# The second element's h on ScalarE's queue, and its transposition ahead of the sixth output product

## The chip, the cores and the metric

The kernel runs on one core of a Trainium2 chip. The metric is the device time of one execution in microseconds (us), as the median of several runs. The core's engines are named as the profile names them: PE is TensorE (PEld its weight loads), DVE is VectorE, ACT is ScalarE, POOL is GpSimd, and SP is SyncE, whose queue only issues transfers here.

## The reference

The input x holds 64 elements (graphs) of 256 nodes with 512 features in float32; adj is one 256 x 256 adjacency matrix for all of them. Two layers follow each other.

```python
# layer 0
mi = x @ Wi.T;  mj = x @ Wj.T          # W = [Wi | Wj], 512 x 1024
h = layernorm(x + deg * (mi + b) + a @ mj)
# layer 1: attention of 8 heads of 64, masked by adj
q, k, v = h @ Wq.T + bq, h @ Wk.T + bk, h @ Wv.T + bv
attn = softmax(where(adj == 0, -inf, q k^T / 8))
out = layernorm(h + (attn v) @ Wo.T + bo)
```

Each element is independent of the others. h of an element, 256 x 512, is needed in two forms: with nodes on the partitions, as the sum to which layer 1 is added (the tile xh), and with features on the partitions, as the operand of the products for q, k and v (the tile hT).

## The kernel before

**Pairs.** The elements are worked in pairs (NB = 2), numbered g; b1 is a pair's first element and b2 its second. A product with one of Wq, Wk, Wv, Wo for a pair is a 512 x 512 by 512 x 512 product, split into 2 x 2 blocks and done with seven block products in place of eight, after a scheme with sums of blocks. The lists o, q, k, v hold these seven steps each (o for the output product with Wo of pair g, the others for pair g+1). Each step is eight matmuls into one bank of PSUM and then the reading of that bank by another engine. Blocks of the left operand are quarters of hT (or of aoT, the attention's result), and their four sums hS (or oS), which DVE makes in four steps (L477 to L480). The right operands, blocks or sums of blocks of the weights, are not kept: each step takes the next `factor` tile, which SP's queue has loaded from DRAM, eight ahead. The order of these loads follows the list `queue`.

**Banks.** The steps share three PSUM banks, taken in turn (tile `st`, or `po` in layer 0). Step 1 and step 3 of a product go to one bank: step 1 is read out to a kept tile (u), and then step 3 adds to the same bank. So PE may start step 3 only when u has been read. The second and third entries of each list are exchanged (`second_late`), so that o[1], q[1] and k[1] are such third steps.

**One pass of the main loop** (g from 0 to 30) works on pair g's attention and output product, and in between on layer 0 of pair g+1, whose steps come from `layer0`. The last part of the pass, around the change, is

```python
run([o[0], neighbours, take1, take0, q[0], give1, send1, o[1], k[0], give0, send0, multiply,
     *left_steps(oS[g], in_order), q[1], k[1]])
run(o[2:6] + work[SLOTS + 2] + [v[0], o[6], v[1]])
```

Here `neighbours` is the product with the graph for b2 of pair g+1, `take1` and `take0` add it and take the statistics of the norm for the two halves of 128 nodes, and `give1` and `give0` apply the norm on ACT (L466 makes the shift, L467 scales the half of xh): after L467 the half is h. `send1` and `send0` are calls of `send_h` for the two halves, and `work[SLOTS + 2]` is one call of `turn_h`.

**The way of h from xh to hT** has four steps. `send_h` writes each half of h to DRAM, in blocks of 128 columns (tile h_cols, one transfer of 256 KB a half, L599). After the second half it reads all of it back as 512 KB (tile hB, L603), so that a DVE transposition of 32 x 32 blocks (`turn_h`, L485, in `transposed`) gives hT. For a pair's second element `turn_h` then makes the sums hS. hT's second half is first needed by q[2], the sums by q[3].

**Order.** A scheduler places each engine's instructions. Those wrapped in `in_order` (all of PE's, and many others) stay on their engine in the order in which they are written; others it places where it expects them to be ready. An engine and a queue work their instructions off in the order that results. All transfers are issued by SP's queue.

**Reading the banks here.** k[0] is read by ACT as `u<-st,bk`, q[1] as `qT<-st,bq`, k[1] as `kT<-st,bk` (L711, two instructions each). Each of o[2] to o[6] is read by DVE at L740, which adds it to xh; that of o[5] is twice as long, as it is added in two places.

Of the kernel before, what the change touches and what calls it, by code (L numbers as in the profile page):

```python
# [16 lines left out]
P = 128  # L17
# [207 lines left out]
def unshifted_path(ctx, tc, flag, x, adj, wiT, wjT, b0, wqT, bq, wkT, bk, wvT, bv, woT, bo, out):  # L225
# [16 lines left out]
    nc = tc.nc  # L242
# [4 lines left out]
    R = 32  # L247
    NB = 2
    NG = B // NB
    H = D // 2  # L250
    SLOTS = NB * NC // 2
# [44 lines left out]
    xh = {}  # L296

    def load_x(b):
        if b < B:
            xh[b] = p6.tile([P, NT, D], F32, tag="xh", name="xh")  # L300
            nc.sync.dma_start(out=xh[b], in_=x[b].rearrange("(t p) d -> p t d", p=P))

    b_bc = p4.tile([P, D], F32, tag="u", name="b_bc")
    xB, hB = {}, {}
# [37 lines left out]
    a = p2.tile([P, NT, N], F32, tag="pe", name="a")  # L342
# [30 lines left out]
    def add_bias(b):  # L373
        in_order(nc.gpsimd.tensor_tensor(xh[b], xh[b], degb, ALU.add))
# [101 lines left out]
    def left_steps(f, order=anywhere):  # L476
        return [lambda: order(nc.vector.tensor_add(f["S1"], f["A21"], f["A22"])),  # L477
                lambda: order(nc.vector.tensor_sub(f["S2"], f["S1"], f["A11"])),  # L478
                lambda: order(nc.vector.tensor_sub(f["S3"], f["A11"], f["A21"])),
                lambda: order(nc.vector.tensor_sub(f["S4"], f["A12"], f["S2"]))]  # L480
# [112 lines left out]
    h_cols = {}  # L593

    def send_h(b, t):
        i = b % NB
        if t == 1:
            h_cols[b] = dram.tile([D // P, N, P], F32, tag=f"h{i}", name="h_cols")
        nc.sync.dma_start(out=h_cols[b][:, t * P:(t + 1) * P, :].rearrange("q p n -> p q n"),  # L599
                          in_=xh[b][:, t, :].rearrange("p (q n) -> p q n", n=P))  # L600
        if t == 0:
            hB[b] = p1.tile([P, N // R, P], F32, tag="hB", name="hB")
            nc.sync.dma_start(out=hB[b].rearrange("p a n -> p (a n)"),  # L603
                              in_=h_cols[b].rearrange("q (r a) n -> (q r) (a n)", r=R))

    def turn_h(b):
        g, i = divmod(b, NB)
# [60 lines left out]
    def second_late(steps):  # L668
        return [steps[0], steps[2], steps[1], *steps[3:]]
# [30 lines left out]
    def qk_steps(g, store, tag, bias, diff, early=False):  # L700

        def new_store():
            store[g] = p1.tile([P, NC, NB * N], F32, tag=tag, name=tag)

        def place(i, j):
            return store[g][:, 2 * j:2 * j + 2, i * N:(i + 1) * N]

        def biased(b):
            def evict(dst, ps):
                for m in range(2):  # L710
                    nc.scalar.activation(dst[:, m, :], ps[:, m, :], AF.Identity, bias=b[:, m:m + 1], scale=1.0)  # L711
            return evict

        def last(dst, ps, addend):
            for m in range(2):
                nc.vector.scalar_tensor_tensor(dst[:, m, :], ps[:, m, :], diff[:, m:m + 1],
                                               addend[:, m, :], ALU.add, ALU.add)

        return qkv_steps(g, True, new_store, place, biased(bias), biased(diff), last, early)

    def v_steps(g, early=False):
        def new_store():
            vv[g] = p1.tile([P, NB, NT, D], F32, tag="v", name="v_sb")

        def place(i, j):
            return vv[g][:, i, :, j * H:(j + 1) * H]

        def copy(dst, ps):
            nc.scalar.copy(dst, ps)

        return qkv_steps(g, False, new_store, place, copy, copy, nc.vector.tensor_add, early)
# [59 lines left out]
    def scores(g, w):  # L791


        i, pr = divmod(w, NC)
        n0 = i * N
        ps = score_banks("ps").rearrange("p j (t q) -> p j t q", t=NT)
        for kc in range(NT):
            for j in range(2):
                rows = slice(j * DH, (j + 1) * DH)
                matmul(ps[:, j, kc, :], kT[g][rows, pr, n0 + kc * P:n0 + (kc + 1) * P],  # L800
                       qT[g][rows, pr, n0:n0 + N], start=True, stop=True)

        def exponentials():
            pe = p2.tile([P, 2, NT, N], F32, tag="pe", name="pe")
            nc.vector.tensor_add(  # L805
                pe.rearrange("p j t q -> p j (t q)"), ps.rearrange("p j t q -> p j (t q)"),
                maskT.rearrange("p t q -> p (t q)").unsqueeze(1).to_broadcast([P, 2, NT * N]))
            flat = pe.rearrange("p j t q -> p (j t q)")
            in_order(nc.scalar.activation(flat, flat, AF.Exp, scale=QSCALE,  # L809
                                          accum_out=etot[:, NB * g + i, pr:pr + 1]))  # L810
            pk = p3.tile([P, 2, N], F32, tag="pk", name="pk")
            nc.gpsimd.tensor_tensor(pk, pe[:, :, 0, :], pe[:, :, 1, :], ALU.add)  # L812
            made[g, w] = pe, pk

        return exponentials
# [10 lines left out]
    def values(g, w):  # L826
        i, pr = divmod(w, NC)
        if w == 0:
            aoT[g] = p1.tile([P, NC, NB * N], F32, tag="aoT", name="aoT")
            oS[g] = pair_blocks(aoT[g], "oS")  # L830
        pp = w % 2
        if pp == 0:
            pavs[g] = value_bank("pav").rearrange("p (r q) -> p r q", r=2)
        pe, _ = made[g, w]
        for kc in range(NT):
            for j in range(2):
                h0 = (2 * pr + j) * DH
                matmul(pavs[g][j * DH:(j + 1) * DH, pp, :], vv[g][:, i, kc, h0:h0 + DH], pe[:, j, kc, :],
                       start=(kc == 0), stop=(kc == NT - 1))

    def multiply():
        while products:
            d, spread = products.pop()
            in_order(nc.gpsimd.tensor_tensor(d, d, spread, ALU.mult))

    def divide_two(g, w):

        dst = target(g, w)
        nc.scalar.copy(dst, pavs[g])
        divide(dst, [made.pop((g, w - 1))[1], made.pop((g, w))[1]])  # L850
# [44 lines left out]
    def layer0(g):  # L895

        b1, b2 = NB * g, NB * g + 1

        def item(f, *args):
            return lambda: f(*args)  # L900

        p, q = l0_steps(b1), l0_steps(b2)
        return [p[:3] + [item(turn_x, b2)] + p[3:4],
                p[4:7] + [item(sum_x, b2), item(add_bias, b2)] + q[:1],
                p[7:10], p[10:] + q[1:3],
                q[3:6] + [item(turn_h, b1)] + q[6:7],
                q[7:], [item(turn_h, b2)]]

    def run(steps):
        for s in steps:  # L910
            s()
# [4 lines left out]
    def order_of(name):  # L916
        return [(name, n) for n in RIGHT]

    for g in range(-1, NG - 1):
        o, q, k, v = (order_of(name) for name in ("wo", "wq", "wk", "wv"))  # L920
# [18 lines left out]
    p, q = l0_steps(0), l0_steps(1)  # L939
# [18 lines left out]
    o = second_late(qk_steps(0, qT, "qT", bq_sb, bqd, True))  # L958
    k = second_late(qk_steps(0, kT, "kT", bk_sb, bkd, True))
    v = second_late(v_steps(0, True))  # L960
# [21 lines left out]
    for g in range(NG - 1):  # L982
        load_x(NB * (g + 2))
        load_x(NB * (g + 2) + 1)
        work = layer0(g + 1)
        run(work[0])
        for w in range(2, NB * NC, 2):
            values(g, w - 2)
            values(g, w - 1)
            multiply()  # L990
            divide_two(g, w - 1)
            scores(g, w)()
            if w == 4:
                run(work[2])
            later = scores(g, w + 1)
            later()
            run(work[w // 2 if w < 4 else w // 2 + 1])
        w = NB * NC - 2
        values(g, w)
        values(g, w + 1)  # L1000
        multiply()
        o = o_steps(g)
        q = second_late(qk_steps(g + 1, qT, "qT", bq_sb, bqd))
        k = second_late(qk_steps(g + 1, kT, "kT", bk_sb, bkd, True))
        v = second_late(v_steps(g + 1, True))
        neighbours, take1, take0, give1, send1, give0, send0 = work[SLOTS + 1]
        divide_two(g, w + 1)
        run([o[0], neighbours, take1, take0, q[0], give1, send1, o[1], k[0], give0, send0, multiply,
             *left_steps(oS[g], in_order), q[1], k[1]])
        run(o[2:6] + work[SLOTS + 2] + [v[0], o[6], v[1]])  # L1010
        end = finish_steps(g)
        k = with_output_bias(g + 1, k)[2:]
        run(q[2:5] + end[:1] + q[5:6] + end[1:2] + q[6:7] + end[2:3] + k[:1] + end[3:4] + k[1:] + end[4:] + v[2:3])
        turn_x(NB * (g + 2))
        sum_x(NB * (g + 2))
        if g + 2 < NG:
            add_bias(NB * (g + 2))
        run(v[3:5])
        run([scores(g + 1, 0), scores(g + 1, 1)])
        run(v[5:])  # L1020
# [93 lines left out]
```

## Time and profile before

| | |
|---|---|
| median of 3 runs | 3117.25 us (3113.67 to 3117.7) |
| the profiled execution: its span, first to last instruction | 3114.5 us |
| TensorE's granted clock in it | 0.999 |
| PE busy | 3066.7 us (98%) |
| DVE, ACT, POOL busy | 71%, 31%, 48% |
| transfers of h_cols, hB | 124 of 256 KB, 62 of 512 KB, all issued by SP |
| from issue to landing, median | h_cols 2.4 us, hB 3.6 us |

The profiled execution has no other time of its own than the span; what lies around it is in the runs' times alone. Times in the profile's views are counted from the span's start. In a timeline a line has the start, the length, the engine, the source line and the operation with its tiles; instructions of one kind that follow each other are merged (x2, x8), and a bracket gives the idle time before them and what ended it. In a list of waits the columns are the sum, the number and the longest. SPq and ACTq mean the engine's queue, in which transfers are issued. Line numbers are those of the kernel before; in the changed kernel those from L599 on stand two lines later.

### The profile page before, as it was taken

Reading aid. Unit: us, or ns where it says so; the run is one execution under the profiler, and the core shown is the slowest. Engines: PE = TensorE matmul, PEld = TensorE weight load, DVE = VectorE, ACT = ScalarE, POOL = GpSimd, SP = SyncE. Lnnn points to the kernel's source line nnn. Section 1 sums busy time; section 2 is a strip of 40 time slices with the busy share of each in tenths; the row PEclk is TensorE's granted clock in tenths of the full one; section 3 lists DMA queues with packets and bytes.
Section 4 is the critical chain, followed back from the end, with each engine's and each line's share of the span. In section 5 each row is a group of like instructions: output and inputs, shape, how many; then the busy total and the mean of one; then the engine's idle time right before and its main releaser. Section 6 shows DMA issues by size and latency. Waiting matters only on the chain. (4 is left out here: it accounts for less than half of the span.)

```text
span 3114.5 us, 42683 instructions
## 1 busy us (share of the span) xinstructions
PE 3066.7 (98%) x14598; PEld 2125.4 (68%) x14598; DVE 2200.1 (71%) x3298; ACT 967.4 (31%) x1861; POOL 1505.3 (48%) x1255
## 2 busy tenths in 40 slices
PE   8999999999999999999999999999999999999998
PEld 4667766677766777666776667776677766677665
DVE  6776677766777767777667776677766777767775
ACT  2322333323333323332233332333332333323332
POOL 2544445544545445454454554454543545445453
PEclk9999999999999999999999999999999999999999
DMA  7355544455444555345553445544455444555333
GB/s 253 116 151 156 166 122 131 133 155 165 143 123 125 157 165 152 117 129 151 156 166 119 129 135 158 164 142 124 124 159 164 144 123 125 158 158 158 119 106 103
DMA packets 410395, 447.28 MB, mean 144 GB/s; under 512 B 40896, under 2 KB 300224, under 8 KB 409792
## 3 DMA queue, kind: packets, MB, share of 16 engines
q1 hardware_dynamic: 410176, 444.50, 48.4%
q8 instruction: 120, 1.97, 0.3%
q14 instruction: 99, 0.81, 0.1%
HBM read 340.79 MB, written 70.25 MB: 132 GB/s over the span
## 5 line engine op out<-in xcount | busy, mean ns | idle before, releaser
L461 POOL TENSOR_TENSOR rstd<-ve,mhalf 128x1 f32<-128x1 f32 x256 | 140.4, 552 | 715.8 <-DVE below L459 715.8
L812 POOL TENSOR_TENSOR pk<-pe 128x512 f32<-128x512 f32 x256 | 322.5, 1276 | 327.6 <-ACT pe L809 327.5
L290 PE MATMUL po<-w,xS 128*128 128x512 f32 x1024 | 462.4, 599 | 0.4 <-DVE xS L478 0.4
L290 PE MATMUL st<-hS,factor 128*128 128x256 f32 x2048 | 453.5, 380 | 5.1 <-DVE xh L740 3.8
L290 PEld LDWEIGHTS st<-hS,factor 128*128 128x128 f32 x2048 | 388.9, 190 | 60.1 <-DVE xh L740 6.4
L809 ACT ACTIVATE pe<-pe 128x1024 f32<-128x1024 f32 x256 | 270.9, 1058 | 379.0 <-DVE pe L805 379.0
L290 PE MATMUL po<-w,xT 128*128 128x512 f32 x768 | 354.5, 605 | 13.1 <-DVE xT L485 11.1
L290 PE MATMUL st<-hT,factor 128*128 128x256 f32 x1536 | 352.6, 380 | 0.7 <-ACT hT L622 0.7
L290 PEld LDWEIGHTS po<-w,xS 128*128 128x128 f32 x1024 | 190.1, 191 | 235.9 <-issue 206.4
L805 DVE TENSOR_TENSOR pe<-ps,maskT 128x1024 f32<-128x1024 f32 x256 | 298.1, 1195 | 35.3 <-PE ps L290 35.3
L290 PEld LDWEIGHTS st<-hT,factor 128*128 128x128 f32 x1536 | 292.2, 190 | 41.7 <-ACT hT L622 0.9
L882 DVE RECIPROCAL rden<-den 128x256 f32<-128x256 f32 x127 | 223.1, 1757 | 92.2 <-PE den L290 89.0
L290 PEld LDWEIGHTS po<-w,xT 128*128 128x128 f32 x768 | 144.7, 192 | 181.2 <-issue 163.3
L290 PE MATMUL ps<-qT,kT 64*128 64x256 f32 x2048 | 265.0, 393 | 0.0
L290 PE MATMUL pav<-pe,v_sb 128*64 128x256 f32 x2048 | 250.2, 386 | 1.9 <-ACT pe L809 1.8
L883 POOL TENSOR_TENSOR rtot<-rtot,rden 128x256 f32<-128x256 f32 x127 | 92.3, 727 | 329.7 <-DVE rden L882 329.7
L740 DVE TENSOR_TENSOR xh<-st,xh 128x512 f32<-128x512 f32 x186 | 144.6, 777 | 136.4 <-PE st L290 136.4
L290 PEld LDWEIGHTS pav<-pe,v_sb 128*64 128x64 f32 x2048 | 135.3, 136 | 154.0 <-issue 95.4
L290 PEld LDWEIGHTS ps<-qT,kT 64*128 64x128 f32 x2048 | 184.7, 187 | 77.8 <-issue 51.3
L290 PE MATMUL st<-factor,hS 128*128 128x256 f32 x1024 | 234.8, 383 | 0.0
L525 POOL TENSOR_TENSOR lo<-mj,hi 128x512 fp32r<-128x512 f32 x128 | 175.2, 1378 | 107.3 <-ACT hi L524 107.3
L290 PE MATMUL st<-factor,oS 128*128 128x256 f32 x992 | 224.3, 380 | 0.0
(115 smaller groups left out, 4679.5 us busy)
## 6 DMA issues: line engine op xcount, KB each, us to landing
xB<-in_x_dram SPq DMA_DIRECT2D x256, 128.0 KB, 3.8
xh<-in_x_dram SPq DMA_DIRECT2D x64, 512.0 KB, 4.2
factor<-wq SPq DMA_DIRECT2D x128, 256.0 KB, 4.3
factor<-wk SPq DMA_DIRECT2D x128, 256.0 KB, 3.0
factor<-wv SPq DMA_DIRECT2D x128, 256.0 KB, 2.7
spread<-rden SPq DMA_DIRECT2D x1016, 32.0 KB, 1.9
factor<-wo SPq DMA_DIRECT2D x124, 256.0 KB, 3.2
h_cols<-xh SPq DMA_DIRECT2D x124, 256.0 KB, 2.4
```

The lines of the kernel that those rows point to most:

```text
L290: in_order(nc.tensor.matmul(*args, **kw))
L461: nc.gpsimd.tensor_tensor(rstd, ve, mhalf, ALU.pow)
L525: nc.gpsimd.tensor_tensor(k["lo"][:, t, :], k["mj"][:, t, :], k["hi"][:, t, :].bitcast(F32), ALU.subtract)
L740: nc.vector.tensor_add(dst, src, dst)
L805: nc.vector.tensor_add(pe.rearrange("p j t q -> p j (t q)"), ps.rearrange("p j t q -> p j (t q)"), maskT.rearrange("p t q -> p (t q)").uns ...
L809: in_order(nc.scalar.activation(flat, flat, AF.Exp, scale=QSCALE, accum_out=etot[:, NB * g + i, pr:pr + 1]))
L812: nc.gpsimd.tensor_tensor(pk, pe[:, :, 0, :], pe[:, :, 1, :], ALU.add)
L882: nc.vector.reciprocal(rden, den)
L883: nc.gpsimd.tensor_tensor(rtot, rtot, rden, ALU.add)
```

## The change

For a pair's second element, the two writes and the read of `send_h` are issued by ACT instead of SP, and are kept in the written order of ACT's instructions. The first element's stay on SP as they were. And the call of `turn_h` moves from behind o[5] to in front of it.

```diff
         if t == 1:
             h_cols[b] = dram.tile([D // P, N, P], F32, tag=f"h{i}", name="h_cols")
-        nc.sync.dma_start(out=h_cols[b][:, t * P:(t + 1) * P, :].rearrange("q p n -> p q n"),
-                          in_=xh[b][:, t, :].rearrange("p (q n) -> p q n", n=P))
+        queue_of = nc.scalar if i == NB - 1 else nc.sync
+        in_order_of = in_order if i == NB - 1 else anywhere
+        in_order_of(queue_of.dma_start(out=h_cols[b][:, t * P:(t + 1) * P, :].rearrange("q p n -> p q n"),
+                                       in_=xh[b][:, t, :].rearrange("p (q n) -> p q n", n=P)))
         if t == 0:
             hB[b] = p1.tile([P, N // R, P], F32, tag="hB", name="hB")
-            nc.sync.dma_start(out=hB[b].rearrange("p a n -> p (a n)"),
-                              in_=h_cols[b].rearrange("q (r a) n -> (q r) (a n)", r=R))
+            in_order_of(queue_of.dma_start(out=hB[b].rearrange("p a n -> p (a n)"),
+                                           in_=h_cols[b].rearrange("q (r a) n -> (q r) (a n)", r=R)))
...
-        run(o[2:6] + work[SLOTS + 2] + [v[0], o[6], v[1]])
+        run(o[2:5] + work[SLOTS + 2] + [o[5], v[0], o[6], v[1]])
```

In the built program this is the order on ACT in each of the 31 passes; the lines with a plus are new, the others as before:

```
  shift, xh      L466, L467: first half of h
+ h_cols<-xh     first write
  u<-st,bk x2    reads k[0]
  shift, xh      second half of h
  qT<-st,bq      reads q[1], first half
+ h_cols<-xh     second write
  qT<-st,bq      second half
  kT<-st,bk x2   reads k[1]
+ hB<-h_cols     the read, which waits until both writes have landed
  u<-st          reads v[0]
```

On DVE the transposition `hT<-hB` stands in front of the long L740 (that of o[5]) instead of behind it; the sums of hS follow that L740 as before. The orders of PE and POOL are the same. SP's has the three transfers less.

## The prediction

> **What bounds the kernel now.** I read the page's first part, then the waits of TensorE (PE), then the timeline of one pass on each engine.
>
> ```profile
> span 3114.5 us, 42683 instructions
> ...
> PE 3066.7 (98%) x14598; PEld 2125.4 (68%) x14598; DVE 2200.1 (71%) x3298; ACT 967.4 (31%) x1861; POOL 1505.3 (48%) x1255
> ```
>
> PE is busy 98%: it sets the end, and only what makes PE wait, or stops making it wait, counts. Its waits are few (total, times, longest):
>
> ```profile
> PE pa L290 <- POOL lo L525: 15.9, 31, 0.5
> PE po L290 <- DVE xT L485: 11.1, 2, 8.3
> PE st L290 <- DVE xh L740: 3.8, 5, 1.2
> ```
>
> The first is a constant 0.5 us in each of 31 passes, the second belongs to the start. Only the third lies in the change's place. In the trace a pass takes 95.73 to 95.8 us from one first `st<-factor,oS` product to the next, except for seven of 30, longer by 0.1 to 1.8 us. Six of them are those in which VectorE (DVE) waits for hB (`DVE hT L485 <- DMA hB<-h_cols: 5.5, 6`, in the waits). Summing each product's delay over its best pass gives 5.8 us: **all that an earlier h can win**.
>
> The pass that starts at 1209.36 is a usual one. DVE (start, length):
>
> ```profile
> 1213.01 0.69 DVE L740 TENSOR_TENSOR xh<-st,xh 128x512 f32<-128x512 f32 x1 [1.04 <-PE st L290]
> 1214.74 1.23 DVE L740 TENSOR_TENSOR xh<-st,xh 128x1024 f32<-128x1024 f32 x1 [1.03 <-PE st L290]
> 1215.88 2.09 DVE L485 STREAM_TRANSPOSE hT<-hB 128x1024 f32<-128x1024 f32 x1
> ...
> 1220.54 0.68 DVE L740 TENSOR_TENSOR xh<-st,xh 128x512 f32<-128x512 f32 x1
> ```
>
> Behind the transposition come the four sums of hS (1218.00 to 1220.62) and the last L740, for o[6]. Its end, 1221.23, frees the bank of q[3], whose weights load at 1221.28: no room. SyncE's queue (SP), which issues the transfers:
>
> ```profile
> 1204.86 0.38 SPq L599 DMA_DIRECT2D h_cols<-xh  x1
> 1205.33 0.46 SPq L442 DMA_DIRECT2D factor<-in_woT_dram  x1
> 1205.88 0.44 SPq L442 DMA_DIRECT2D factor<-in_wvT_dram  x1
> 1206.41 0.43 SPq L442 DMA_DIRECT2D factor<-wq  x1
> 1206.93 0.38 SPq L599 DMA_DIRECT2D h_cols<-xh  x1
> ...
> 1211.52 0.33 SPq L603 DMA_DIRECT2D hB<-h_cols  x1
> ```
>
> The second write's 512-byte packets start only at 1209.4, behind three factor loads of the same queue, and it lands 4.6 us after its issue, where the first needed 2.4. The read lands at 1215.3, 0.6 us before DVE takes it. ScalarE (ACT) and PE in this place:
>
> ```profile
> 1204.02 0.81 ACT L467 ACTIVATE xh<-xh,shift,rstd 128x512 f32<-128x512 f32 x1
> 1204.74 0.82 ACT L711 ACTIVATE u<-st,bk 128x256 f32<-128x256 f32 x2
> 1205.45 0.29 ACT L466 ACTIVATE shift<-below,rstd 128x1 f32<-128x1 f32 x1
> 1205.77 0.81 ACT L467 ACTIVATE xh<-xh,shift,rstd 128x512 f32<-128x512 f32 x1
> 1206.49 0.82 ACT L711 ACTIVATE qT<-st,bq 128x256 f32<-128x256 f32 x2
> 1207.83 0.84 ACT L711 ACTIVATE kT<-st,bk 128x256 f32<-128x256 f32 x2 [0.53 <-PE st L290]
> ```
>
> ```profile
> 1202.45 5.34 PE L290 MATMUL st<-hT,factor 128*128 128x256 f32 x24
> 1207.63 1.89 PE L290 MATMUL st<-factor,aoT 128*128 128x256 f32 x8
> ```
>
> The 24 products are k[0], q[1], k[1], eight each, 0.2157 us apart: k[1] starts at 1202.45 + 16 x 0.2157 = 1205.90, its weights at 1205.69. It adds to the bank that u(bk) empties, so it must wait for u(bk), which ends at 1205.56: **0.13 us of room**. ACT is 31% busy on the page, but here it runs back to back.
>
> **What the Trainium skill says.** "Perfetto Trace Analysis", section "DMA Instruction — HWDGE (DVE, Sync)": such an instruction is profiled from the moment its semaphores are met, and only at its end is the sequencer free for the next. The trace agrees on SP: h writes take 366 to 384 ns and the next issue starts after them (1204.86, then 1205.33). "DMA: Bandwidth & Descriptors", section "Queues, rings and completion order": SP and ACT each own a row of rings on the same 16 DMA engines, and an engine alternates between rows packet by packet. All 444.50 MB of the data went through one queue, so no run here shows this yet.
>
> **The change part by part.**
>
> 1. *First h write on ACT,* between L467 and u(bk). It waits for L467, which ends at 1204.83; a wait of ACT for itself costs 0.034 us (shift to xh in the trace). Then 0.37 us of issue, taken from SP's row since ACT issues no transfer before. So u(bk) starts at 1205.24, or 1205.32 with the 0.08 us that lie between SP's issues, instead of 1204.74: 0.50 to 0.58 later. PE's room takes 0.13 to 0.2 (at the weights, and a little in the pipeline: in late passes a bank freed 0.28 us late cost 0.24). Left: 0.30 to 0.45 us a pass; I take 0.38, times 31 = **+11.8 us**. Bounds: 0 if the issue overlaps ACT's work; about 0.8 x 31 = 25 us if it is twice as dear as on SP.
> 2. *Second write on ACT.* L467 now ends at about 1207.1. The write is behind the first half of qT, whose execution it can overlap; issue near 1207.15, 0.2 later than now. The rest of qT ends by 1208.0; the bank is needed at 1209.14. Cost 0, hidden by 1.1 us of slack; at an issue of twice the length still 0.
> 3. *hB's read on ACT,* behind kT. It holds ACT until the second write has landed; behind it stands only the copy of v[0]'s bank, not before 1216.46. Cost 0 unless it waits some 5 us.
> 4. *SP loses three transfers,* 93 x 0.36 = 33 us of issue and the waits on xh and h_cols. Its factor loads move up by 0.5 to 1.7 us; they run eight ahead, so PE gains nothing. POOL issues no transfer and keeps its order.
> 5. *Landing of h.* In a queue of its own the second write no longer stands behind the loads; its 512 packets, 27 ns each in the trace, need 512/16 x 27 ns = 0.9 us alone, up to 1.8 if every second packet is another's. From 1207.15 plus 0.8 to the first packet it lands near 1210.0 to 1210.5 (now 1211.5). The read then takes 3.6 to 4.4 us, because factor loads run beside it: 1213.8 to 1215.0.
> 6. *Transposition ahead of o[5]'s L740.* The earliest start is behind L740 of o[4], 1213.01 + 0.69 = 1213.70 (plus 0.38 for PE's shift). But what follows grows by that L740, 1.14 us: hB must land by 1215.88 - 1.14 = 1214.74, or 1215.1 with PE 0.38 later, where 1215.9 sufficed. By step 5 a usual pass meets it: the 5.8 us go. I leave 1.5 us for late passes. o[5]'s own bank is wanted only by q[2] at 1219.5; freed near 1217.3 it costs 0.
>
> Sum: 11.8 - 5.8 + 1.5 = +7.5 us on the profiled 3114.5, so 3122.0. The median of the runs, 3117.25, lies 2.75 above this span, so I expect **3125** us as a median.
>
> **The rivals.**
>
> *The issue on ACT is hidden (not slower).* If ACT's sequencer issues the transfer while ACT is still inside L467, or in under 0.1 us, u(bk) keeps its place and only the gain is left: 3117.25 - 5.8 = 3111.5, with a part of the stall up to 3119. It decides at about 0.15 us of delay to u(bk). For it: ACT's low busy share. Against: the write needs all of L467, and the row of 0.37 us.
>
> *hB lands too late for its new place.* If the two queues only share the bandwidth and the read lands when it does now (median 6.2 us after the pass's first oS product, 1215.55), it misses 1215.1 by 0.43 us in most passes: 13.3 us, and the late passes cost their 5.8 again. 3117.25 + 11.8 + 13.3 = 3142. For it: the 16 DMA engines are busy at 0.75 to 1.1 of their time, by the trace's packets, from 1206 to 1211. Against: they are nearly idle around 1204 and 1212, and h waits for a place in the queue, not for bandwidth. It decides at a landing of 1215.1.
>
> *ACT's issue is dearer than SP's,* 0.8 us: 3117.25 + 25 - 5.8 = 3137. For it, nothing but that ACT's issue is not on record.
>
> *The change does not do what it says:* the built order has the transfers on ACT and the transposition one place earlier in all 31 passes, so no.
>
> **How the numbers follow.** A measurement here can tell about 0.2% from no change, 6.2 us: below 3111.0 is faster, above 3123.5 slower. Forecast 0.58, own range 3120 to 3129, two thirds of it above the bound (0.40 slower, 0.18 same). Hidden issue 0.20 (0.17 same, 0.03 faster: its full gain is just under the bound). Late hB 0.17 and dear issue 0.05, slower. Together 0.03, 0.35, 0.62. The range leaves out the full gain and the worst of late hB: 3113 to 3137.
>
> **What would show it.** Right: a new PE wait of `st` on ACT's u(bk), 31 times, 0.2 to 0.4 us; PE's wait on L740 gone or nearly; u(bk) 0.5 us behind the end of L467 with the issue between; the transposition starting within 0.1 us of its predecessor's end; writes landing under 3.5 us after issue. Wrong: no wait on u(bk) (hidden issue), or DVE waiting for hB in most passes (late hB), or an issue row far from 0.37 us. A time under 3113 breaks step 1, one over 3137 steps 1 or 5.

## The result, and the profile after

The changed kernel took 3128.88 us (median of 5 runs, 3126.03 to 3130.18), the kernel before 3116.09 us beside it (5 runs, 3113.67 to 3117.7): a ratio of 1.0049, 95% interval 1.0036 to 1.0061. It is slower by 12.8 us; 3125 was forecast. The profiled span grew from 3114.5 to 3126.6 us, by 12.1. Where they lie, read from the starts of the passes: 30 passes are longer by 0.36 us on average (10.8), the start up to the first pass is longer by 1.8 (0.4 of it the same stall; the rest lies in the loading of the start, where the kernels shown here differ by up to 4 us), and the end is shorter by 0.6.

The waits of PE and of its weight loads (PEld) after the change:

```profile
PE pa L290 <- POOL lo L525: 15.8, 31, 0.5
PE po L290 <- DMA w<-in_wiT_dram: 9.3, 1, 9.3
PE st L290 <- DVE xh L742: 3.0, 5, 1.1
```

```profile
PEld st L290 <- ACT u L713: 15.8, 31, 0.5
PEld st L290 <- DVE xh L742: 6.5, 9, 1.5
```

The constant wait for `lo` is as before, and the 9.3 us for the first weights stand where the start waited 11.1 us for xT. The new thing is in the second list only: 31 weight loads wait for u(bk), one in each pass. PE's own list does not have it, because a matmul is shown 0.38 us long while they follow each other every 0.2157 us; a gap that pushes the next one by 0.27 us leaves only 0.1 us of idle time to see. ACT's timeline in the pass that starts at 1215.82:

```profile
1210.12 0.81 ACT L467 ACTIVATE xh<-xh,shift,rstd 128x512 f32<-128x512 f32 x1
1210.96 0.37 ACTq L601 DMA_DIRECT2D h_cols<-xh  x1
1211.37 0.84 ACT L713 ACTIVATE u<-st,bk 128x256 f32<-128x256 f32 x2 [0.44 <-ACT xh L467]
...
1213.14 0.45 ACT L713 ACTIVATE qT<-st,bq 128x256 f32<-128x256 f32 x1
1213.27 0.37 ACTq L601 DMA_DIRECT2D h_cols<-xh  x1
1213.68 0.47 ACT L713 ACTIVATE qT<-st,bq 128x256 f32<-128x256 f32 x1
```

The first issue begins 0.03 us after L467 ends and is 0.37 us long, and u(bk) starts 0.04 us behind it: 1.25 us after L467's start, where it was 0.72 us before. The second issue runs while the first half of qT is still at work. PE in the same place:

```profile
1208.97 2.78 PEld L290 LDWEIGHTS st<-hT,factor 128*128 128x128 f32 x13
1212.26 1.59 PEld L290 LDWEIGHTS st<-hT,factor 128*128 128x128 f32 x8 [0.51 <-ACT u L713]
```

The eight loads of k[1] stand 0.51 us behind their predecessors. From the starts of the matmuls, the first of k[1] comes 0.485 us after the one ahead of it and the second 0.320 us after that, in place of 0.2157 each: 0.374 us of PE lost, in each of 31 passes, **11.6 us**.

The second half of the change, on DVE:

```profile
1219.47 0.69 DVE L742 TENSOR_TENSOR xh<-st,xh 128x512 f32<-128x512 f32 x1 [1.04 <-PE st L290]
1220.86 2.08 DVE L485 STREAM_TRANSPOSE hT<-hB 128x1024 f32<-128x1024 f32 x1 [0.70 <-DMA hB<-h_cols]
1222.85 1.18 DVE L742 TENSOR_TENSOR xh<-st,xh 128x1024 f32<-128x1024 f32 x1
```

The transposition now stands between the two L742, and waits for hB; in the whole run that wait is `DVE hT L485 <- DMA hB<-h_cols: 33.0, 29, 3.5`, where it was 5.5 us in 6 passes. Mostly PE does not feel it. But eight passes are still late at q[3], by 0.2 to 2.2 us, together 5.4 us; before they were seven with 5.8.

### The profile page after: what moved, and what is told of

Same layout as the page of the kernel before. It is cut to its first block, busy times and chain, and to the rows that moved or that the text cites. A ratio compares the mean times of both kernels' runs of the same rounds, so it can differ in the third digit from the quotient of the medians.

```text
span 3126.6 us, 42655 instructions
## 1 busy us (share of the span) xinstructions
PE 3075.8 (98%) x14598; PEld 2118.7 (68%) x14598; DVE 2194.7 (70%) x3298; ACT 974.4 (31%) x1861; POOL 1505.4 (48%) x1255
## 5 line engine op out<-in xcount | busy, mean ns | idle before, releaser
L290 PE MATMUL st<-hT,factor 128*128 128x256 f32 x1536 | 360.9, 381 | 4.5 <-ACT hT L624 0.7
L742 DVE TENSOR_TENSOR xh<-st,xh 128x512 f32<-128x512 f32 x186 | 143.3, 770 | 115.7 <-PE st L290 115.7
```

The source lines that it names most:

```text
L290: in_order(nc.tensor.matmul(*args, **kw))
L742: nc.vector.tensor_add(dst, src, dst)
```

## The experiments

All ratios are against the kernel before, run beside each kernel on the same chip. For all rows below the first two it took 3111.4 to 3111.5 us, against 3116.1 above, probably because hB was seldom late there (no trace of it from those chips was taken); the differences count. In the table times of h are those of the pair's second element, medians over the 31 passes, counted from the pass's first `st<-factor,oS` product; "read" is the time from hB's issue to its landing; "late" is the sum over 30 passes of what each is longer than the shortest. Each trace is of one run and not of the median: in those of e1 and e2 the kernel took 3114.8 and 3120.6 us, in those of e3 and e4 3155.9 and 3134.3.

| kernel | us | ratio, 95% interval | shortest pass | second write lands | read | hB lands | late |
|---|---|---|---|---|---|---|---|
| before (first comparison) | 3116.09 | | 95.73 | 2.40 | 3.75 | 6.24 | 6.7 |
| after (first comparison) | 3128.88 | 1.0049 (1.0036 to 1.0061) | 96.11 | 0.98 | 4.24 | 5.34 | 6.1 |
| e1_move_only | 3118.03 | 1.0022 (1.0012 to 1.0032) | 95.73 | 2.24 | 3.26 | 5.60 | 7.2 |
| e2_queue_only | 3122.49 | 1.0035 (1.0023 to 1.0047) | 96.11 | 0.95 | 4.25 | 5.19 | 0.9 |
| e3_first_write_sp | 3151.99 | 1.0127 (1.0111 to 1.0142) | 96.18 | 2.49 | 4.37 | 6.92 | 31.0 |
| e4_first_write_sp_no_move | 3129.69 | 1.0055 (1.0042 to 1.0069) | 95.75 | 2.65 | 4.15 | 7.35 | 24.9 |
| e5_write_behind_u | 3132.90 | 1.0071 (1.0058 to 1.0085) | 96.04 | 1.86 | 4.25 | 6.27 | 13.2 |
| e5b_write_behind_u_no_move | 3114.57 | 1.0013 (1.0005 to 1.0021) | 95.74 | 1.81 | 4.42 | 6.40 | 5.9 |
| e6_two_issues_no_move | 3138.55 | 1.0084 (1.0070 to 1.0098) | 96.64 | 0.22 | 4.32 | 4.61 | 0.8 |
| e8_first_write_act_only | 3122.66 | 1.0033 (1.0021 to 1.0045) | 96.11 | 0.89 | 3.24 | 4.26 | 0.6 |
| e9_sp_behind_k0 | 3109.49 | 0.9994 (0.9985 to 1.0002) | 95.77 | 1.26 | 3.27 | 4.55 | 0.0 |
| e10_first_act_behind_u_move | 3113.32 | 1.0006 (1.0000 to 1.0013) | 95.73 | 1.32 | 4.14 | 5.47 | 4.5 |
| e10b_first_act_behind_u | 3109.56 | 0.9997 (0.9989 to 1.0005) | 95.73 | 1.24 | 4.13 | 5.42 | 1.1 |
| after_same_chip | 3126.36 | 1.0050 (1.0036 to 1.0063) | 96.10 | 1.00 | 4.20 | 5.32 | 5.2 |

Where every pass of a kernel is late (e3, e5), its shortest pass is already above 95.73, so "late" leaves a part out there. In the full change, e2, e6 and e8 it is the stall at u(bk) that lengthens the shortest pass.

### The two parts alone, and the first write put back

e1 has only the second hunk of the change (`o[2:5] + work[SLOTS + 2] + [o[5], ...]`). e2 has only the first.

> Only the transposition is put ahead of o[5]'s L740; all transfers stay on SP. Theory (the loss is ACT's issue of the first write in front of u(bk), 0.375 us of PE in each of 31 passes; the transposition's new place needs hB by about 5.5 us after the pass's first oS product): no PE wait for u(bk), but hB lands when it does before (mean 6.3 us), so DVE waits for it in nearly every pass and PE loses about 0.8 us a pass: +20 us on before, about 3136. Rival A (the transposition's earlier place is the whole loss, ACT's issue is free): the same loss as the full change, +12 us, 3129, or more. Rival B (two queues in contention are the loss): no queue is added, so no loss, 3116 or the gain of 5 us.

> Only the three transfers go to ACT's queue; the transposition stays behind o[5]'s L740. Theory: the PE wait for u(bk) stays, +11.6 us; hB lands at about 5.4 us in a pass, where 6.7 is enough, so the late passes of before mostly go, -5: about 3123 (+7). Rival A: no loss, 3111 (-5). Rival B: as the full change, 3129.

The stall belongs to the queue part: e2's passes are all about 0.4 us longer than before's shortest (the matmuls' starts give a stall of 0.374 us in each), and none is late. Of PEld's waits:

```profile
PEld st L290 <- ACT u L713: 15.7, 31, 0.5
```

It lost 11.1 us in the median, 4 more than forecast, probably because before had few late passes to win on this chip. e1 has no such wait and loses 6.6 us, not 20: hB was read in 3.26 us here instead of 3.75 and landed at 5.60, near the limit for the early place. Rival A, that the move is the whole loss, falls with these two. Rival B, contention of two queues, falls only in part: e1 loses without a second queue, and e2 has the wait for u(bk) in every pass, but its time alone would fit both (+12 was forecast by rival B for it). What decides is e5b below, which has the same three transfers on ACT and loses 3 us.

e3 and e4 keep the first write on SP; e3 has the transposition in front, e4 behind.

```diff
-        queue_of = nc.scalar if i == NB - 1 else nc.sync
-        in_order_of = in_order if i == NB - 1 else anywhere
+        queue_of = nc.scalar if i == NB - 1 and t == 0 else nc.sync
+        in_order_of = in_order if i == NB - 1 and t == 0 else anywhere
```

> The full change, but the first half's write stays on SP; the second write and the read are on ACT, the transposition is ahead of o[5]'s L740. Theory: u(bk) is again straight behind xh, so PE's wait for it is gone (0 instead of 0.375 us a pass). PE is then 0.375 us earlier against h, and hB, at about 5.5 to 5.7 us, is just late for the new place: 0.2 us a pass and the late ones, together 8 to 9 us, against 5.8 before: about 3119 (+3). Rival A: 3129, since the transposition is where it was. Rival B: 3129 less a third.

> As the last, and the transposition behind o[5]'s L740 as before the change. Theory: no wait for u(bk), and hB at about 5.5 to 5.7 us where 6.7 is enough: nearly all of the 5.8 us of late passes go: about 3112 (-4), the fastest of the four. Rival A: the same, 3111. Rival B: slower than before, 3124 or so, as most of the traffic is still on a second queue.

Both were far slower than the theory said: against before, e4 lost 18 us and e3 40, the slowest of all. The stall at u(bk) was indeed gone from the waits. What came instead, in e3's waits of DVE and of PE:

```profile
DVE hT L485 <- DMA hB<-h_cols: 83.5, 31, 4.3
```

```profile
PE st L290 <- DVE xh L742: 32.2, 38, 1.4
```

The second write was on ACT's own queue and was issued even 0.3 us earlier than by SP before, yet landed no sooner: 2.49 us against 2.40. In the trace its first packet moves 2.6 us after the issue (median of 31, 1.6 to 3.2), when most of the factor loads of SP's queue have gone through (71% of the bytes of the three, in the median). SP's queue in that pass, which starts at 644.07:

```profile
639.57 0.38 SPq L601 DMA_DIRECT2D h_cols<-xh  x1
640.04 0.47 SPq L442 DMA_DIRECT2D factor<-in_woT_dram  x1
640.60 0.44 SPq L442 DMA_DIRECT2D factor<-in_wvT_dram  x1
641.13 5.18 SPq L442 DMA_DIRECT2D factor<-wq  x4
```

As before the change, the first write makes SP wait for xh until 4.5 us ahead of the pass, and three loads then follow in one burst, just ahead of the second write. In the full change woT is issued 2.6 us and wvT 1.9 us earlier against the pass (0.37 of this is the later start of the pass). So a second theory: **h lands when the burst of loads in front of it is over, whichever queue it stands in; what brought it forward in the full change was that SP no longer waited with the first write.** And the read is slower here (4.15 and 4.37 us) than in before and e1 (3.75 and 3.26). There it stood in SP's queue and held back the loads behind it; here two of these are issued ahead of it, 0.2 and 1.9 us into the pass, and move beside it. Whether the queue itself matters is seen in e10.

### The issue behind u(bk), the issue doubled, and the first write alone

e5 and e5b call `send1` behind `k[0]`, so that u(bk) goes ahead of the issue; e5b has the transposition behind o[5].

```diff
-        run([o[0], neighbours, take1, take0, q[0], give1, send1, o[1], k[0], give0, send0, multiply,
+        run([o[0], neighbours, take1, take0, q[0], give1, o[1], k[0], send1, give0, send0, multiply,
```

> The full change, with the first write on ACT placed behind u(bk) instead of in front of it (send1 is called behind k[0]). Theory 1 (the loss is the 0.37 us issue standing between xh and u(bk)): PE's wait for u(bk) is gone. Theory 2, from the run with the first write on SP (h's landing follows the backlog of factor loads, which the first write on SP holds back by waiting for xh; not the queue in which h stands): SP is free of the first write here, so the second write lands near 1 us in the pass and hB near 5.5 to 5.7, about at the limit of 5.5 for the transposition's early place: 0 to 0.3 us a pass lost. Together 0 to +8 us on before, not +12. Rival (a second queue in itself is slow, so that the run with the first write on SP lost 40 us because of it): as there, +30 us or more.

> As the last, and the transposition behind o[5]'s L740 as before the change. Theories 1 and 2: no wait for u(bk), hB before 6.7 us in nearly every pass: what remains of late passes in before goes, -1 to -6 us by the chip: the only version that should beat before. Rival (second queue slow in itself): +10 to +18 us, as the run with the first write on SP and the old place of the transposition.

The first theory held: PEld's wait for u(bk) is gone in both. That a second queue is slow in itself, which forecast +10 to +18 us for e5b, is not so: it lost 3. ACT's timeline of e5 shows why an issue need not cost ACT anything:

```profile
1208.36 0.81 ACT L467 ACTIVATE xh<-xh,shift,rstd 128x512 f32<-128x512 f32 x1
1209.08 0.45 ACT L713 ACTIVATE u<-st,bk 128x256 f32<-128x256 f32 x1
1209.20 0.37 ACTq L601 DMA_DIRECT2D h_cols<-xh  x1
1209.44 0.46 ACT L713 ACTIVATE u<-st,bk 128x256 f32<-128x256 f32 x1
```

The issue runs beside the first half of u(bk), and the second half starts 0.36 us after the first, as it did before. But both kernels missed their numbers. The second write landed at 1.8 to 1.9 us, not near 1, and hB at 6.3 to 6.4. A part of this is the origin: with the stall gone PE is 0.37 us earlier in the pass against h, so the 0.98 us of the full change would read 1.35 here. The rest is 0.5 us. The write goes out 0.13 us later by the same count (the scheduler put the first half of qT in front of the second L467), but that is not the reason: e10b below issues it in the same place on SP, and there it lands at 1.24. In e5 its packets take 2.36 us from the first to the last, in e10b 1.80: the load that SP issues 0.5 us after it lands at 1.84 in e5, ahead of the write, and at 1.98 in e10b, behind it (medians). In the early place (e5) a landing at 6.3 is late in nearly every pass, +21 us; in the old place (e5b) only now and then, +3 us. e5 against e5b, with hB landing alike, is the price of the early place: 18 us. e5b did not beat before.

e6 is e2 with the first write in two transfers of 128 KB:

```diff
+        parts = 2 if i == NB - 1 and t == 1 else 1
+        for part in range(parts):
+            qs = slice(part * NC // parts, (part + 1) * NC // parts)
```

> The three transfers on ACT, the transposition behind o[5]'s L740, and the first write split in two transfers of 128 KB, both between xh and u(bk): the suspected cost doubled, the bytes unchanged. Theory 1: u(bk) is another 0.41 us late (0.37 and the 0.04 between issues), all of it PE's, as PE's room of 0.13 us is used up by the first: 0.78 us a pass, 24 us on before, where the one issue cost 11 in the run with only the queue changed. Rival (the loss comes from the transfers' traffic or from the second queue, not from ACT's time): about as with one issue, +11.

It lost 27.1 us. ACT, then PE's waits:

```profile
1214.07 0.89 ACTq L604 DMA_DIRECT2D h_cols<-xh  x2
1215.00 0.84 ACT L716 ACTIVATE u<-st,bk 128x256 f32<-128x256 f32 x2 [0.97 <-ACT xh L467]
```

```profile
PE st L290 <- ACT u L716: 19.3, 31, 0.7
```

Two issues hold u(bk) for 0.97 us where one held it for 0.44, and the shortest pass goes from 95.73 to 96.11 to 96.64: 0.38 for the first issue and 0.53 for the second, which is its full time with the gap, since PE's room is used up. With the same bytes, the loss follows the number of issues. Now PE's own list shows the wait too, because the gap has grown beyond a matmul's shown length.

e8 has only the first write on ACT, in its place ahead of u(bk) (condition `i == NB - 1 and t == 1`).

> Only the first write is on ACT, in front of u(bk); the second write and the read are on SP, the transposition behind o[5]'s L740. Theory 1: the wait for u(bk) stays, +11.6 us, less what late passes before has: +6 to +11. Theory 2: though the second write stands in SP's queue, behind the factor loads, it lands near 1 us in the pass (2.4 in before), since the loads ahead of it are issued about 1 us sooner; the read lands near 4.7 to 5.2. Rival to theory 2 (a queue of its own is what lets h land early): the second write lands near 2.2 to 2.4 us as before.

The pass is again 96.11, and the second theory is met: on SP, behind the loads, the second write landed at 0.89 us, as early as on ACT (0.95 to 1.00), and the read took 3.24 us, so that hB was there at 4.26, 0.9 us before e2, which differs only in having the second write and the read on ACT. SP's queue in the pass that starts at 1213.78 has the load of wvT 5.3 us ahead of the pass, where e3 has it 3.5 us ahead:

```profile
1208.50 0.42 SPq L442 DMA_DIRECT2D factor<-in_wvT_dram  x1
1210.15 0.34 SPq L442 DMA_DIRECT2D factor<-wq  x1
1211.23 0.37 SPq L601 DMA_DIRECT2D h_cols<-xh  x1
```

The four cases side by side: with the first write on SP the second lands at 2.40 us (on SP, before) or 2.49 (on ACT, e3), with the first on ACT at 0.89 (on SP, e8) or 0.95 (on ACT, e2); 0.37 us of the difference is the later start of the pass. And in all the kernels but e5 and e5b (1.4 us) the second write lands 0.66 to 0.79 us (medians) behind the landing of the last load issued ahead of it, on either queue.

### Without ACT, and with the better places together

e9 is the kernel before with `send1` called behind `k[0]` (as in the diff above) and nothing else: all of h on SP.

> The kernel before, all on SP and the transposition in its old place, but send1 is called behind k[0]: in SP's order one factor load (woT) passes in front of the first write, which waits for xh. Theory 2 (h's second write starts when the loads ahead of it are through, wherever it stands): one load of the three moves up by 1.5 us, so the second write lands about 0.5 to 0.9 us sooner than in before and hB too; nothing is added on ACT. Late passes mostly go: -1 us on a chip where before is at 3111, up to -5 where it is at 3117. Rival (a queue of its own is needed): no difference from before.

> The transposition ahead of o[5]'s L740 as in the full change; only the first write is on ACT, behind u(bk); the second write and the read are on SP. Theory 1: no wait for u(bk). Theory 2: the second write lands near 1.0 to 1.4 us in the pass, and the read, which stands ahead of the later loads in SP's own queue, needs 3.3 us instead of the 4.1 to 4.4 on ACT's: hB near 4.6 to 5.0, before the 5.5 that the early place needs. So the transposition's move costs nothing and the time is that of the next kernel within 2 us: -1 to +2 on before. Rival (the early place costs by itself): +5 or more.

> As the last with the transposition behind o[5]'s L740. Theories 1 and 2: no wait for u(bk), hB near 4.6 to 5.0 where 6.7 is enough: all late passes go, the floor of 95.73 us in each pass: -1 us on a chip where before is at 3111, -5 where it is at 3117. Rival (any issue on ACT here costs PE): +5 to +11.

> The full change again, beside the others. By the parts measured so far (11.6 us for the issue in front of u(bk), hB's read slower on ACT's queue, so that some passes miss the early place) +12 to +15 us on before.

In e9 one load passes in front of the first write, and this is enough: hB lands at 4.55 us, no pass is late, all 30 take 95.77 us. It is 2 us below before, and the interval includes 1: on a chip where before is at 3111 there is nothing more to win; whether it wins 5 us on one where before is at 3117 was not tried. e10b is the same within the measurement; its second write, on SP, is issued at the same place as e5b's on ACT and lands 0.57 us sooner (1.24 against 1.81). e10, the only difference being the transposition in front, is 3.8 us slower than e10b: hB lands at 5.47 here, not at 4.6 to 5.0 (in SP's built order a further load stands ahead of the read, which took 4.14 us), and nine passes miss the early place. e10 and e10b also show that the slow read is not a matter of ACT's queue: in both it is on SP, behind one load issued about 1.2 us ahead of it. The read's time goes with what moves beside it. By the packets (medians), 46 to 58 KB of other transfers move between its first and last packet in e1, e8 and e9, where it takes 3.2 to 3.3 us, 136 KB in before (3.75 us), and 217 to 258 KB in e10, e10b, e2 and the full change, where it takes 4.1 to 4.25 on either queue. None of the versions with the early place beat its sibling with the old one. The full change itself, run again here, lost 14.9 us, as was expected.

## Why the prediction was right, and in which term it was not

The direction, the place and the main term were right; a smaller term of the sum was not. The time came to lie 0.1 us inside the upper end of the range (two of the five runs lie outside it), and the change, +12.8 us, was well above the forecast +7.75.

- **What bounds (PE, no slack at q[3], 0.13 us at u(bk)):** right. Both places are where PE lost time in the passes, in every trace in which it did.
- **Step 1, the issue ahead of u(bk), +11.8 us:** measured 11.6, by 0.374 us in 31 passes. The parts: 0.37 us of issue as on SP, 0.04 behind it (0.00 to 0.08 was allowed), u(bk) 0.53 later (0.50 to 0.58). The Trainium skill, "Perfetto Trace Analysis", section "DMA Instruction — HWDGE (DVE, Sync)", has the sequencer free for the next instruction only at the end of the issue's row, and e6 agrees: its two rows fill 0.89 us and u(bk) starts 0.04 us behind them. e5 shows that work handed over earlier runs on beside an issue. The sign for this step was given wrongly: the wait stands under PEld, not PE.
- **Steps 2 and 3, no cost:** right; in e2, with both on ACT, the stall of 0.374 us is all that its passes have over before's.
- **Step 4, SP's loads move up, of no use to PE:** right for PE directly, but it was the working part: it, not the queue, brought h forward (e3, e8).
- **Step 5, landing:** its reason failed. "In a queue of its own the second write no longer stands behind the loads" is contradicted by e3. Its number was a little early: the second write was to land at 1210.0 to 1210.5, or 0.6 to 1.1 us in the pass; measured 0.98 in a pass whose start is itself 0.37 late, 1.35 by the same origin. Its first packet moved 1.3 us after the issue, where 0.8 was assumed. The Trainium skill, "DMA: Bandwidth & Descriptors", section "Queues, rings and completion order", says that an engine alternates between rows packet by packet. In the full change 260 KB of SP's loads move between the first and the last packet of the second write, but with the write on SP as well it is as much (e8, 258 KB), so no run here shows the alternation as such. Nor does a transfer of the second queue start at once: 2.6 us in e3. What holds it until then was not settled.
- **Step 6, -5.8 + 1.5 for late passes:** this term was mis-sized. 5.8 became 5.4, so 0.4 was won and not 4.3. hB did land earlier, at 5.34, which is 5.71 by before's origin, instead of 6.24; but the early place asks for it 1.1 us earlier. The prediction had it land at 4.4 to 5.6 and the limit at 5.74, so the usual pass was left with next to no room. Beside the start this is why more was lost than forecast: 11.6 - 0.4 + 1.4 at the start - 0.6 at the end is 12.0, and the span grew by 12.1.
- **The rivals:** the hidden issue did not happen where the write stood, and did where it was placed behind u(bk) (e5). Late hB came in part: its sign, DVE waiting for hB in most passes, is there (29 waits), though PE was late in eight passes only; in e3 and e5 it came in full (31 waits, and nearly every pass late). Three signs of being right did not appear: the transposition did not follow its predecessor at once, PE's wait on DVE's reading did not go (3.0 us in 5 passes, from 3.8 in 5), and the writes took 3.9 and 3.5 us to land. A dearer issue is excluded by the row of 0.37 us.

## What to carry to other kernels

An engine that is idle two thirds of the time can still have no room at one place: before a transfer's issue is put on it, look at what stands behind in its order and how late that may be, and put the issue behind the reading that frees a bank, not ahead of it. The transfer that landed late here was helped by an earlier issue of the loads ahead of it, and not by another queue, where later loads could run beside it (e5): ask which wait holds the issuing queue back and bunches the loads behind it. And work set earlier in an order moves the time by which its input is needed; price that against when the input lands in every pass, not in the usual one.

## What the runs showed of the hardware that was not expected

- A 256 KB write issued by ACT while loads of SP's queue were in flight moved its first packet 2.6 us after its issue (e3), no sooner than in SP's own queue (2.5 us before); ACT's first write in the full change landed 3.9 us after its issue, where SP's took 2.4.
- The 512 KB read took 3.2 to 3.3 us with 46 to 58 KB of other transfers beside it (e1, e8, e9) and 4.1 to 4.25 us with 217 to 258 KB, whether on SP's queue (e10, e10b) or on ACT's (e2, the full change).
- An issue on ACT placed behind u(bk) ran beside u(bk)'s activations, which had been handed over before it (e5: 0.37 us, and u(bk) no later than before); placed ahead of u(bk) it put u(bk) off by 0.53 us (the full change).
- The read in SP's unchanged order took 3.75 us in the trace of before and 3.26 in that of e1, from another comparison. Whether the chip, the run or the moved transposition makes the difference is not shown; the full change's read took 4.24 and 4.20 us in two comparisons.
